# Seven block products in place of eight for the GRU gates of a 64-graph kernel, with block sums on GpSimd and tiles updated in place

## Chip, cores and metric

The kernel runs on one core of one Trainium2 chip. The metric is the device time of one execution in microseconds (us). All runs told of here were in the fast state. A profile of one execution gives the engines' instructions; its "span" is a little shorter than the device time. "Clock" is the share of TensorE's full clock that was granted, and "half clock" is a share of 0.5.

## What is computed

There are 64 graphs of 256 nodes with 256 features, all in fp32. Cut to what matters:

```python
x_conv = relu(bn(conv17(relu(bn(conv1(x))))) + x)           # along the nodes
A = exp(-dist(x @ w_se.T)) * adj
x_nmp = A @ relu(x @ w_msg.T + b_msg)
gi = concat([x_conv, x_nmp]) @ w_ih.T + b_ih                # 512 -> 768
gh = x @ w_hh.T + b_hh                                      # 256 -> 768
r, z = sigmoid(gi_r + gh_r), sigmoid(gi_z + gh_z)
n = tanh(gi_n + r * gh_n)
x1 = layernorm(x + (1 - z) * n + z * x)
h = layernorm(x1, gamma, beta)
out = layernorm(2 * x1 + relu((adj @ h) @ W_rel + b_rel + h @ W_root))
```

## The kernel before

It works in eight rounds of eight graphs. While a round's graphs go through gates, update and aggregation, the convolution of the next round (Winograd-like: many elementwise steps on VectorE, then products on TensorE) is cut into pieces and put between them by `pump()`. The order is made by hand: it is the order in which the program gives each engine, and SyncE, which issues the loads, its instructions.

```python
def load_x(k):                      # on SyncE, like the convolution's weights w
    XG[k] = work.tile([P, C, D], F32, tag="x", name="x")                  # 2 buffers
    nc.sync.dma_start(out=XG[k], in_=x[k].rearrange("(c p) d -> p c d", p=P))

def gates_rz(k, n):                 # n: half of the nodes
    q, ins = inputs(k, n)
    prz = bank("ps_rz")             # one PSUM bank, 512 columns
    for c in range(C):
        nc.tensor.matmul(prz, XT[k][:, c, q], whh[:, c, 0:2 * D], start=(c == 0), stop=False)
    for i, t in enumerate(ins):     # 2 of the convolution, 2 of the messages
        nc.tensor.matmul(prz, t, wih[:, i, 0:2 * D], start=False, stop=(i == 3))
    nc.vector.tensor_add(rz[:, n, :], prz, brzn[:, :2 * D])
    nc.scalar.activation(rz[:, n, :], rz[:, n, :], AF.Tanh, scale=0.5)
# gates_n(k, n): the same with 256 columns for each of gi_n and gh_n ...

def update(k):
    ...
    w = work.tile([P, C, D], F32, tag="w", name="w", bufs=1)
    nc.vector.tensor_sub(w, XG[k], nn)          # the last reader of XG[k]
    ...
    X1[k] = work.tile([P, C, D], F32, tag="x1", name="x1", bufs=2)

# the loop over a round's graphs
    load(k + 3)
    load_x(k + 1)                               # ahead of this graph's convolution weights
    gates_rz(k, 0); pump(); gates_n(k, 0); step(y_left); pump()
    transposes_h(k - 1); pump()                 # its first matmuls mark the stretches below
    gates_rz(k, 1); pump(); passing(k + 1); pump(); factors(k + 2)
    gates_n(k, 1); pump(); project(k - 1)
    ...                                         # update(k), distances, messages, mask
    agg = aggregate(k - 1)                      # y = max(y, 0) + X1[k - 1], late in graph k
```

Of the kernel before, what the change touches and what calls it, by code (L numbers as in the profile page):

```python
# [12 lines left out]
F32 = mybir.dt.float32  # L13
# [16 lines left out]
BG = 8  # L30
NB = B // BG
PI = math.pi

# [41 lines left out]
def gnn_two_layers(  # L75
# [22 lines left out]
    def bank(name):  # L98
        return psum.tile([P, 512], F32, tag="ps", name=name)

    def stt(o, in0, s, in1, op0=ALU.mult, op1=ALU.add):
        nc.vector.scalar_tensor_tensor(o, in0, s, in1, op0=op0, op1=op1)  # L102
# [24 lines left out]
    tb_dram = nc.inline_tensor(np.ascontiguousarray(tb), name="tap_matrix")  # L127
    tap_sb = const.tile([TAPS * OB, NM * OB], F32)
    nc.scalar.dma_start(out=tap_sb, in_=tb_dram.ap())
    mhalf = const.tile([P, 8], F32)  # L130
# [36 lines left out]

    def filters(pool):
        W2[0] = pool.tile([P, C, NM, D], F32, name="w2all")
        pieces, groups = [], []  # L170
# [251 lines left out]
    def conv(b):  # L422
# [97 lines left out]

        xcs = [work.tile([P, C, 4, N], F32, tag="xc", name="xc", bufs=3) for _ in range(2)]

        def channels(q):
            for o in range(C):
                ps = bank("ps_xc")
                for j in range(4):
                    nc.tensor.transpose(ps[:, j * P:(j + 1) * P], X[:, V + 4 * q + j, o * P:(o + 1) * P], ident)  # L527
                pv = ps.rearrange("p (j g t) -> p j g t", j=4, g=BG)
                for h in range(2):
                    nc.scalar.activation(  # L530
                        xcs[h][:, o].rearrange("p g (t j) -> p j g t", j=M)[:, 4 * q:4 * q + 4],
                        pv[:, :, 4 * h:4 * h + 4, :], AF.Relu)
                yield 1.0
# [13 lines left out]
        for g in range(BG):  # L547
            XC[b * BG + g] = (xcs[g // 4], g % 4)


    XG, ADJ, XT, NMP, AT, MSG, X1, H, ST, RZ, OUTS = ({} for _ in range(11))

    def load(k):

        if k >= B:
            return
        XT[k] = work.tile([P, C, N], F32, tag="xT", name="xT", bufs=4)
        nc.sync.dma_start(out=XT[k], in_=xt_dram[k // 2][:, :, (k % 2) * N:(k % 2 + 1) * N])
        ADJ[k] = work.tile([P, C, N], F32, tag="adj", name="adj", bufs=5)
        nc.sync.dma_start(out=ADJ[k], in_=adjT[k].rearrange("(c p) n -> p c n", p=P))  # L560

    def load_x(k):
        if k < B:
            XG[k] = work.tile([P, C, D], F32, tag="x", name="x")
            nc.sync.dma_start(out=XG[k], in_=x[k].rearrange("(c p) d -> p c d", p=P))

    def messages(k):
        MSG[k] = work.tile([P, C, D], F32, tag="msg", name="msg", bufs=3)
        st = work.tile([P, C, 4], F32, tag="st", name="st", bufs=3)
# [37 lines left out]
    def mask(k):  # L607
        nc.vector.tensor_mul(AT[k], AT[k], ADJ[k])
# [9 lines left out]

    def inputs(k, n):
        xc, g = XC[k]  # L620
        q = slice(n * P, (n + 1) * P)
        return q, (xc[:, 0, g, q], xc[:, 1, g, q], NMP[k][:, 0, q], NMP[k][:, 1, q])

    def gates_rz(k, n):
        if n == 0:
            RZ[k] = (work.tile([P, C, 2 * D], F32, tag="rz", name="rz", bufs=1),
                     work.tile([P, C, 2 * D], F32, tag="gn", name="gn", bufs=1))
        q, ins = inputs(k, n)
        prz = bank("ps_rz")
        for c in range(C):  # L630
            nc.tensor.matmul(prz, XT[k][:, c, q], whh[:, c, 0:2 * D], start=(c == 0), stop=False)  # L631
        for i, t in enumerate(ins):
            nc.tensor.matmul(prz, t, wih[:, i, 0:2 * D], start=False, stop=(i == 3))  # L633
        rz = RZ[k][0]

        nc.vector.tensor_add(rz[:, n, :], prz, brzn[:, :2 * D])  # L636
        nc.scalar.activation(rz[:, n, :], rz[:, n, :], AF.Tanh, scale=0.5)  # L637

    def gates_n(k, n):
        q, ins = inputs(k, n)  # L640
        pn = bank("ps_n")
        for c in range(C):
            nc.tensor.matmul(pn[:, D:], XT[k][:, c, q], whh[:, c, 2 * D:], start=(c == 0), stop=(c == C - 1))  # L643
        for i, t in enumerate(ins):
            nc.tensor.matmul(pn[:, :D], t, wih[:, i, 2 * D:], start=(i == 0), stop=(i == 3))  # L645
        nc.vector.tensor_add(RZ[k][1][:, n, :], pn, brzn[:, 2 * D:])  # L646

# [5 lines left out]
    def update(k):  # L653

        rz, gn = RZ[k]
        nn = work.tile([P, C, D], F32, tag="nn", name="nn", bufs=1)
        stt(nn, rz[:, :, :D], 1.0, gn[:, :, D:], op0=ALU.add, op1=ALU.mult)
        stt(nn, nn, 0.5, gn[:, :, :D])
        nc.scalar.activation(nn, nn, AF.Tanh)
        yield  # L660

        w = work.tile([P, C, D], F32, tag="w", name="w", bufs=1)
        nc.vector.tensor_sub(w, XG[k], nn)
        stt(w, rz[:, :, D:], 3.0, w, op0=ALU.add, op1=ALU.mult)
        stt(w, nn, 4.0, w)
        mv = work.tile([P, C, 2], F32, tag="mv", name="mv", bufs=4)
        for n in range(C):
            stats(mv, n, w[:, n, :])


        q = work.tile([P, 2, C], F32, tag="q", name="q", bufs=4)
        nc.gpsimd.tensor_scalar(q[:, 0, :], mv[:, :, 1], 4 * EPS, None, ALU.add)  # L672
        nc.gpsimd.tensor_scalar(q[:, 1, :], mv[:, :, 1], 1 + EPS, 4 * EPS * EPS, ALU.mult, ALU.add)
        nc.gpsimd.tensor_tensor(q, q, mhalf[:, :2 * C].rearrange("p (a c) -> p a c", a=2), ALU.pow)
        sh = work.tile([P, C], F32, tag="sh", name="sh", bufs=4)
        nc.gpsimd.tensor_mul(sh, mv[:, :, 0], q[:, 0, :])
        nc.gpsimd.tensor_scalar(sh, sh, -1.0, None, ALU.mult)
        yield
        H[k] = work.tile([P, C, D], F32, tag="h", name="h", bufs=1)
        X1[k] = work.tile([P, C, D], F32, tag="x1", name="x1", bufs=2)  # L680
        for n in range(C):
            nc.vector.tensor_scalar(H[k][:, n, :], w[:, n, :], mv[:, n, 0:1], q[:, 1, n:n + 1],
                                    ALU.subtract, ALU.mult)
        for n in range(C):
            nc.scalar.activation(X1[k][:, n, :], w[:, n, :], AF.Identity, bias=sh[:, n:n + 1], scale=q[:, 0, n:n + 1])
        yield
# [54 lines left out]
    def step(g):  # L741
        if g is not None:
            next(g, None)
# [3 lines left out]
    with tc.tile_pool(name="first", bufs=1) as first_pool:  # L747
# [22 lines left out]

        brzn = const.tile([P, 4 * D], F32)
        nc.sync.dma_start(out=brzn[:, :3 * D], in_=rows[:, R_IH:R_IH + 3 * D].to_broadcast([P, 3 * D]))
        nc.sync.dma_start(out=brzn[:, 3 * D:], in_=rows[:, R_HH + 2 * D:R_HH + 3 * D].to_broadcast([P, D]))
        bhh = first_pool.tile([P, 2 * D], F32, name="bhh")
        nc.sync.dma_start(out=bhh, in_=rows[:, R_HH:R_HH + 2 * D].to_broadcast([P, 2 * D]))
        gb = const.tile([P, 2, C], F32)
        nc.sync.dma_start(out=gb, in_=rows[:, R_GAMMA:R_GAMMA + 2 * D].rearrange("o (v c p) -> p (o v) c", p=P, c=C))
        whh = weight(whhT, D, 3 * D, "whh", nc.sync)

# [10 lines left out]
        for _ in fl:  # L790
            pass
        nc.vector.tensor_add(brzn[:, :2 * D], brzn[:, :2 * D], bhh)
        nc.gpsimd.tensor_scalar(wrr, wrr, 0.5, None, ALU.mult)
# [4 lines left out]
    work = ctx.enter_context(tc.tile_pool(name="work", bufs=2))  # L798
    wih = weight(wihT, 2 * D, 3 * D, "wih", nc.sync, work)
    for k in range(3):  # L800
        load(k)
    load_x(0)
    early = [lambda: messages(0), lambda: messages(1), lambda: factors(0), lambda: distances(0), lambda: mask(0),
             lambda: factors(1), lambda: distances(1), lambda: mask(1), lambda: passing(0), lambda: messages(2)]
    mark = total
# [5 lines left out]
    for f in early:  # L811
        f()

    POINTS = 10
    y_left = None
    for b in range(NB):
# [12 lines left out]
        for k in range(b * BG, (b + 1) * BG):  # L829
            load(k + 3)  # L830
            load_x(k + 1)
            up = update(k)
            agg = None
            gates_rz(k, 0)
            pump()
            gates_n(k, 0)
            step(y_left)
# [3 lines left out]
            pump()  # L841
            gates_rz(k, 1)
            pump()
            if k + 1 < B:
                passing(k + 1)
            pump()
            if k + 2 < B:
                factors(k + 2)
            gates_n(k, 1)
            pump()  # L850
# [20 lines left out]
        for _ in coming:  # L871
            pass
    step(y_left)
    transposes_h(B - 1)
# [47 lines left out]
```

## Time and profile before

| kernel before | |
|---|---|
| median of 3 runs | 2330.31 us (2328.41 to 2331.38) |
| span, mean granted clock | 2326.0 us, 0.988 |
| busy TensorE, VectorE | 2245.9 us, 1685.6 us |
| half clock between the first transposes of h and the last graph | none |

The busy line, the slices, the chain that ended last and the table by stretches stand in the prediction below. A stretch runs from one graph's transposes of h to the next graph's; there are eight in a round, six in which VectorE is busy for 78 to 96% of the time and two in which it is not.

### The profile page before, as it was taken

How to read it: one execution, taken by the hardware profiler on the slowest of the kernel's cores; microseconds unless marked ns; L12 is line 12 of the kernel's file. 1: busy time of each engine (PE TensorE's matmuls, PEld its weight loads, DVE VectorE, ACT ScalarE, POOL GpSimd, SP SyncE). 2: the span in 40 equal slices, each digit the busy share in tenths (PEclk: the TensorE clock that was granted, in tenths of full speed). 3: DMA queues.
4: the chain of work that ended last, by engine and by line, in shares of the span. 5: the costliest groups of instructions: out<-in, count | busy, mean ns of one | idle time of the engine just before them, and what ended most of it. 6: DMA issues, size and time to landing. Idle time of an engine off the chain costs nothing.

```text
span 2326.0 us, 24209 instructions
## 1 busy us (share of the span) xinstructions
PE 2245.9 (97%) x8262; PEld 1474.6 (63%) x8262; DVE 1685.6 (72%) x3212; ACT 768.0 (33%) x1577; POOL 467.2 (20%) x922
## 2 busy tenths in 40 slices
PE   7779999999999999999999999999999999999996
PEld 4565666656666676666766566666666666666663
DVE  3893988659794788839886597956889298874443
ACT  4514322442224322342224432243223532243332
POOL 1000311212122212202212221222222122121211
PEclk9989999999999999999999999999999999999998
DMA  6543252223322144221522233231432214321100
GB/s 176 164 151 113 74 162 73 84 83 127 118 82 100 50 136 131 75 97 48 170 86 73 100 130 124 73 106 53 136 123 81 100 37 158 107 76 36 46 23 14
DMA packets 211088, 226.66 MB, mean 97 GB/s; under 512 B 22047, under 2 KB 201750, under 8 KB 210966
## 3 DMA queue, kind: packets, MB, share of 16 engines
q1 hardware_dynamic: 188408, 191.14, 25.6%
q10 hardware_dynamic: 22558, 33.99, 4.1%
q8 instruction: 66, 1.08, 0.2%
q14 instruction: 56, 0.46, 0.1%
HBM read 179.22 MB, written 45.88 MB: 97 GB/s over the span
## 4 chain that ended last, share of the span: by engine, by line
PE 80%; DVE 13%; DMA 3%; issue 2%; POOL 1%; ACT 1%; ACTq 0%; SPq 0%; POOLq 0%; DVEq 0%
PE ps_rz L633 17%; PE ps_k L382 11%; PE ps_n L645 9%; PE ps_rz L631 8%; PE ps_out L708 8%; PE ps_c L453 5%; PE ps_nmp L615 5%; PE ps_n L643 4%; DVE XF L102 4%; PE ps_out L720 4%; PE ps_msg L573 4%; PE ps_dist L603 2%; DVE w L102 1%; DVE bst L650 1%; PE ps_xc L527 1%
## 5 line engine op out<-in xcount | busy, mean ns | idle before, releaser
L102 DVE SCALAR_TENSOR_TENSOR XF<-XF 128x512 f32<-128x512 f32 (+2 forms) x800 | 506.8, 664 | 7.0
L672 POOL TENSOR_SCALAR q<-mv 128x2 f32<-128x2 f32 x64 | 32.1, 501 | 1476.0 <-DVE mv L651 1476.0
L382 PE MATMUL ps_k<-w,XF 128*128 128x256 f32 x1316 | 296.8, 382 | 4.3 <-ACT AT L605 1.4
L382 PEld LDWEIGHTS ps_k<-w,XF 128*128 128x128 f32 x1316 | 246.7, 190 | 49.2 <-issue 6.4
L646 DVE TENSOR_TENSOR gn<-ps_n,brzn 128x512 f32<-128x512 f32 x128 | 88.1, 688 | 247.5 <-PE ps_n L645 247.5
L637 ACT ACTIVATE rz<-rz 128x512 f32<-128x512 f32 x128 | 80.6, 630 | 512.8 <-DVE rz L636 512.8
L631 PE MATMUL ps_rz<-whh,xT 128*128 128x512 f32 x512 | 240.7, 592 | 0.0
L633 PE MATMUL ps_rz<-wih,xc 128*128 128x512 f32 x512 | 240.7, 592 | 0.0
L633 PE MATMUL ps_rz<-wih,nmp 128*128 128x512 f32 x512 | 240.6, 592 | 0.0
L708 PE MATMUL ps_out<-wrr,hT 128*128 128x512 f32 x512 | 232.9, 598 | 5.5 <-ACT hT L697 5.5
L636 DVE TENSOR_TENSOR rz<-ps_rz,brzn 128x512 f32<-128x512 f32 x128 | 87.6, 684 | 195.9 <-PE ps_rz L633 195.9
L633 PEld LDWEIGHTS ps_rz<-wih,xc 128*128 128x128 f32 x512 | 97.1, 190 | 122.7 <-issue 121.5
L633 PEld LDWEIGHTS ps_rz<-wih,nmp 128*128 128x128 f32 x512 | 97.3, 190 | 122.4 <-issue 122.4
L708 PEld LDWEIGHTS ps_out<-wrr,hT 128*128 128x128 f32 x512 | 98.1, 192 | 105.2 <-issue 93.0
L573 PE MATMUL ps_msg<-wms,xT 128*128 128x260 f32 x512 | 135.7, 405 | 19.0 <-DVE XF L398 11.0
L577 ACT ACTIVATE msg<-msg 128x512 f32<-128x512 f32 x64 | 40.3, 629 | 343.3 <-DVE msg L576 343.3
L631 PEld LDWEIGHTS ps_rz<-whh,xT 128*128 128x128 f32 x512 | 92.2, 190 | 64.5 <-issue 61.2
L643 PE MATMUL ps_n<-whh,xT 128*128 128x256 f32 x512 | 131.6, 379 | 0.0
L645 PE MATMUL ps_n<-wih,xc 128*128 128x256 f32 x512 | 131.4, 379 | 0.0
L645 PE MATMUL ps_n<-wih,nmp 128*128 128x256 f32 x512 | 131.4, 379 | 0.0
L573 PEld LDWEIGHTS ps_msg<-wms,xT 128*128 128x128 f32 x512 | 95.0, 195 | 53.1 <-issue 23.9
L709 ACT COPY hr<-ps_out 128x256 f32<-128x256 f32 x128 | 47.7, 373 | 242.3 <-PE ps_out L708 242.3
(104 smaller groups left out, 3629.0 us busy)
## 6 DMA issues: line engine op xcount, KB each, us to landing
w<-w2m SPq DMA_DIRECT2D x105, 768.0 KB, 5.9
xn<-in_x_dram SPq DMA_DIRECT2D x32, 512.0 KB, 4.6
xt<-xTc ACTq DMA_DIRECT2D x32, 512.0 KB, 3.3
xT<-xt SPq DMA_DIRECT2D x64, 256.0 KB, 3.0
adj<-in_adjT_dram SPq DMA_DIRECT2D x64, 256.0 KB, 2.8
x<-in_x_dram SPq DMA_DIRECT2D x64, 256.0 KB, 3.0
xb<-in_x_dram SPq DMA_DIRECT2D x32, 512.0 KB, 4.3
out_dram<-y ACTq DMA_DIRECT2D x64, 256.0 KB, 2.2
```

The costliest lines, as they stand in the source:

```text
L102: nc.vector.scalar_tensor_tensor(o, in0, s, in1, op0=op0, op1=op1)
L382: nc.tensor.matmul(ps, X[:, slot, c * P:(c + 1) * P], w(m, c), start=(c == 0), stop=(c == C - 1))
L453: nc.tensor.matmul(ps, w1[:, c, o * P:(o + 1) * P], xTc[:, c, :], start=(c == 0), stop=(c == C - 1))
L573: nc.tensor.matmul(ps[:, :D + 4], XT[k][:, c, m * P:(m + 1) * P], wms[:, c, :], start=(c == 0), stop=(c == C - 1))
L615: nc.tensor.matmul(ps[:, d * N:(d + 1) * N], MSG[k][:, m, d * P:(d + 1) * P], AT[k][:, m, :], start=(m == 0), stop=(m == C - 1))
L631: nc.tensor.matmul(prz, XT[k][:, c, q], whh[:, c, 0:2 * D], start=(c == 0), stop=False)
L633: nc.tensor.matmul(prz, t, wih[:, i, 0:2 * D], start=False, stop=(i == 3))
L643: nc.tensor.matmul(pn[:, D:], XT[k][:, c, q], whh[:, c, 2 * D:], start=(c == 0), stop=(c == C - 1))
L645: nc.tensor.matmul(pn[:, :D], t, wih[:, i, 2 * D:], start=(i == 0), stop=(i == 3))
L646: nc.vector.tensor_add(RZ[k][1][:, n, :], pn, brzn[:, 2 * D:])
L708: nc.tensor.matmul(ps, hT[:, c, n * P:(n + 1) * P], wrr[:, c, :], start=(c == 0), stop=(c == C - 1))
L720: nc.tensor.matmul(po, ADJ[k][:, m, n * P:(n + 1) * P], hr[:, m, :], start=False, stop=(m == C - 1), skip_group_check=True)
```

## The change

The intent is to save TensorE time. The gates are a product of a 256-row left side and a 256-row weight, seen as 2 x 2 blocks of 128; a Strassen-type form needs seven block products in place of eight. It needs sums of left blocks (put on GpSimd), differences of weight blocks (once, at the start) and sums of products (VectorE, out of PSUM, where the kernel's banks for TensorE's products lie). To make room, the GRU update works in place, and the convolution's result goes to a ring of 10 graphs. Core of the diff, with cuts:

```diff
 def load_x(k):
-    XG[k] = work.tile([P, C, D], F32, tag="x", name="x")
+    XG[k] = work.tile([P, C, D], F32, tag="x", name="x", bufs=3)
+def blocks(src, s1, s2, s3, s4):
+    a11, a12, a21, a22 = (src[:, c, n * P:(n + 1) * P] for n in range(C) for c in range(C))
+    nc.gpsimd.tensor_add(s1, a21, a22)
+    nc.gpsimd.tensor_sub(s2, s1, a11)
+    nc.gpsimd.tensor_sub(s3, a11, a21)
+    nc.gpsimd.tensor_sub(s4, a12, s2)
+    return a11, a12, s4, a22, s1, s2, s3
+def block_product(k, i, ps, start):        # nmp and xc 384 columns each, x 256
+    for j, (name, w) in enumerate((("nmp", wg[:, i, 1, :]), ("x", wx[:, i, :]), ("xc", wg[:, i, 0, :]))):
+        nc.tensor.matmul(ps[:, :w.shape[-1]], LEFT[k, name][i], w, start=start and j == 0, ...)
+def gates(k):
+    a = bank("ps_a"); block_product(k, 0, a, True)
+    nc.vector.tensor_add(g00, a[:, :HG], bg[:, 1, :])
+    d = bank("ps_d"); block_product(k, 1, d, True)
+    nc.vector.tensor_add(g00, g00, d[:, :HG])
+    yield
+    b_ = bank("ps_b"); block_product(k, 4, b_, True)
+    nc.scalar.copy(g11, b_[:, :HG])
+    c_ = bank("ps_c"); block_product(k, 6, c_, True)
+    nc.vector.tensor_add(g11, g11, c_[:, :HG])
+    yield
+    block_product(k, 5, a, False)              # the fifth, onto bank a: needs the first add to be done
+    nc.vector.tensor_add(<g01 and g10>, <a twice>, bg)
+    ...                                        # products 2 onto b_, 3 onto c_
 def update(k):
-    w = work.tile([P, C, D], F32, tag="w", name="w", bufs=1)
-    nc.vector.tensor_sub(w, XG[k], nn)
+    w = XG[k]
+    nc.vector.tensor_sub(w, w, nn)
     ...
-    X1[k] = work.tile([P, C, D], F32, tag="x1", name="x1", bufs=2)
+    X1[k] = w
...
+    for i, j, l in ((6, 2, 4), (4, 4, 0), (5, 2, 4), (3, 1, 5)):      # at the start
+        for w in (wg, wx):
+            nc.gpsimd.tensor_sub(w[:, i], w[:, j], w[:, l])
```

## The prediction

> **What bounds the kernel now.** I read the page's busy table first, then the slices, then the chain that ended last, and then asked for what no average tells: the busy time of each engine in stretches of one round.
>
> ```profile
> PE 2245.9 (97%) x8262; PEld 1474.6 (63%) x8262; DVE 1685.6 (72%) x3212; ACT 768.0 (33%) x1577; POOL 467.2 (20%) x922
> ...
> PE   7779999999999999999999999999999999999996
> ...
> DVE  3893988659794788839886597956889298874443
> ...
> PE 80%; DVE 13%; DMA 3%; issue 2%; POOL 1%; ACT 1%; ACTq 0%; SPq 0%; POOLq 0%; DVEq 0%
> ```
>
> TensorE is busy 97% of the span, 80% of the final chain is its own work, and the only slices below 9 are the first three (filters, first convolution) and the last. So a microsecond of TensorE work removed from the steady part is worth a microsecond, as long as nothing else takes over. VectorE at 72% looks like room. But its digits swing between 4 and 9, so I cut one round of eight graphs at its eight transposes of h (at 509.92, 535.95 and so on) and asked for the stretches. Columns: us of the stretch; busy us of TensorE, its weight loads, VectorE, ScalarE, GpSimd; clock; DMA.
>
> ```profile
> 509.92:535.95 26.03, 26.03 (x91) 16.26 (x90) 24.87 (x43) 8.38 (x17) 8.31 (x16) 1.00 0.12 41
> 535.95:572.60 36.65, 36.64 (x140) 25.25 (x139) 35.00 (x61) 10.69 (x21) 11.90 (x19) 1.00 0.46 147
> 572.60:616.58 43.98, 42.34 (x163) 29.69 (x162) 37.81 (x82) 9.71 (x20) 7.37 (x14) 1.00 0.42 134
> 616.58:658.42 41.84, 40.98 (x160) 29.10 (x158) 33.69 (x72) 9.71 (x20) 8.03 (x14) 1.00 0.31 104
> 658.42:684.45 26.03, 26.03 (x91) 16.26 (x90) 23.35 (x51) 7.18 (x16) 4.81 (x10) 1.00 0.24 79
> 684.45:713.11 28.66, 28.66 (x115) 18.79 (x114) 25.14 (x47) 12.51 (x27) 9.32 (x18) 1.00 0.21 74
> 713.11:740.89 27.78, 27.78 (x108) 17.96 (x107) 11.86 (x28) 12.81 (x28) 5.62 (x16) 1.00 0.23 76
> 740.89:783.63 42.74, 42.66 (x149) 24.93 (x147) 16.73 (x23) 19.15 (x38) 4.52 (x8) 1.00 0.29 99
> ```
>
> The reader should see two kinds of stretch. In the last two TensorE is full and VectorE is at 43% and 39%. In the first six VectorE is busy 179.9 of 203.2 us, in the first two 96%. Seven of the eight rounds look like this; the last one has no next convolution, VectorE at 46% and 26.03 us per graph.
>
> [...] The trace has two MATMULs per fp32 product and these starts:
>
> ```profile
> 919.12 1.88 PE L631 MATMUL ps_rz<-whh,xT 128*128 128x512 f32 x4
> 920.84 1.88 PE L633 MATMUL ps_rz<-wih,xc 128*128 128x512 f32 x4
> 922.55 1.88 PE L633 MATMUL ps_rz<-wih,nmp 128*128 128x512 f32 x4
> 924.27 1.03 PE L643 MATMUL ps_n<-whh,xT 128*128 128x256 f32 x4
> 925.13 1.03 PE L645 MATMUL ps_n<-wih,xc 128*128 128x256 f32 x4
> ```
>
> Start to start this is 1.716 us per four, 0.429 us each at 512 columns, and 0.2165 us each at 256: linear[...]. [...]
>
> ```profile
> 705.74 1.22 DVE L538 TENSOR_TENSOR XF<-XF,xb 128x1024 f32<-128x1024 f32 x1
> ...
> 705.96 1.05 POOL L582 TENSOR_TENSOR ns<-sq 128x2 f32<-128x2 f32 x1
> ```
>
> A two-element GpSimd sum, 0.19 us when free, took 1.05 us and ended 0.05 us after VectorE's two-input add ended at 706.96. [...]
>
> **Part 1, TensorE.** Before, one graph's gates are 24 instructions of 512 columns and 24 of 256: 24 x 0.429 + 24 x 0.2165 = 15.5 us. After, each of seven products has four of 384 (interpolated 0.323) and two of 256: 1.725 us, times 7 = 12.08; the part of h in the n gate stays, 8 x 0.2165 = 1.73. Sum 13.81. Saved: **1.69 us per graph, 108 us for 64**, all of it on the engine that sets the end. If nothing else moved: 2222 us.
>
> **Part 2, VectorE.** Removed: four evictions of 512 columns (0.686 us each, 2.74) and the two products for h (0.37 each busy, 0.73), which go to ScalarE. Added: the blocks must be summed out of PSUM: five evictions or adds of 384 columns from PSUM and one in SBUF (0.55, between 0.416 at 256 and 0.686 at 512, so 3.3), one of 768 (0.96) and one of 512 (0.69): 4.95. Net **+1.47 us per graph**, 94 us over the run.
>
> **Part 3, GpSimd.** Twelve two-input sums of 128 columns per graph. [...] I take **1.5 us**.
>
> **Part 4, ScalarE.** A copy of 384 columns and two normalisations more, about +1.7 us on a 33% engine: hidden, except that h now goes GpSimd, then ScalarE: about 1 us later.
>
> **Part 5, start.** The new weights need four differences of 768 and four of 256 columns on GpSimd, queued ahead of the first graph's small sums (which ran at 164.6 us) on which its distances, mask and messages hang. [...] **about +12 us**, nothing hidden, since TensorE is idle there. The ring of convolution results and the in-place tiles only free memory.
>
> **Sum.** Crowded six stretches: TensorE 203.2 - 6 x 1.69 = 193.1. VectorE 179.9 + 6 x (1.47 + 1.5) = 197.7, already over TensorE, so these end at about 198 to 200, a gain of 3 to 5 in place of 10. The two light ones gain 3.4. Per round 6.5, seven rounds 45; the last round's eight graphs the full 13.5; the start -12. Gain 46: **2284, say 2285 us**.
>
> **Rivals.** (a) TensorE stays the bound and VectorE's lag is absorbed in the light stretches: 108 less 12 less some waits, 2240 to 2255. For: GpSimd never visibly delayed VectorE before. Against: the new accumulation reuses bank a, so the fifth product waits for VectorE's first eviction some 6 us earlier in TensorE's order, while at the crowded graphs VectorE begins that eviction (of rz) already 6 us after its matmul. TensorE can no longer run far ahead. (b) VectorE becomes the bound[...]: the crowded stretches get longer than before and only light graphs gain, 2310 to 2330. (c) GpSimd's queue delays its own normalisation sums, and h comes late to its transposes, which have only 2 to 4 us to spare at some graphs: same size as (b).
>
> **Range and chances.** Between (a) and (b): 2245 to 2325. A gain of 2% is 2283.7, in the middle of it; the change clearly removes work from the bound, so slower by 2% is remote. Faster 0.47, same 0.49, slower 0.04.
>
> **What would show it.** Gate matmuls at 0.323 us start to start and TensorE busy down by 100 us or so; VectorE busy up by 94 us or more, its two-input instructions longer than 0.69 us at 512 columns where block sums run (this decides between a and b); TensorE waits "from VectorE" or "from GpSimd" in the first stretches of a round, none in the light ones; the first gate matmul at about 200 us, where it was at 188. I am wrong if VectorE's durations do not change and TensorE has no new waits (then 2245), or if block sums take a microsecond each and starve the gates (then above 2325).

The 1.5 us per graph for VectorE held by GpSimd's sums, some 10 of the 12 us of the start, and the size of rival (b) were estimates, and the sum keeps them: it set VectorE at 197.7 us in the six crowded stretches and came to a gain of 46 us, 2285 us. What the trace before does show is a sum on GpSimd that took 0.19 us at 185.19 and 1.05 us at 705.96, beside VectorE's add; that add took 1.22 us, and the mean of such steps of 1024 columns is 1.215, so VectorE was not seen to be held there. ScalarE's 1.7 us can be worked out from the same trace: two normalisations of 0.59 us each, and a copy of 384 columns put at 0.5 from the 0.37 us at 256.

## More of the kernel before

One more view matters later, SyncE's waits before it can issue a transfer (line of the transfer, what it waited for, us in total, times, longest). Before:

```profile
SPq L377 <- DMA w<-w2m: 62.3, 14, 5.0
SPq L565 <- DVE w L663: 59.5, 3, 25.6
```

Line 565 is the load of x. It waited three times in the whole run. Line 377 is the load of the convolution's weights w, which stands behind it in the queue.

## The result

| | before | changed |
|---|---|---|
| median | 2330.85 us (4 runs) | 2413.70 us (4 runs, 2406.36 to 2427.85) |
| span, clock | 2326.0 us, 0.988 | 2404.5 us, 0.965 |
| TensorE busy, idle | 2245.9, 80.1 us | 2190.2, 214.3 us |
| half clock in the steady part | 0 | 81.9 us in 19 stretches |

The ratio is 1.0365 (95% interval 1.0316 to 1.0413): slower, outside the predicted range. A ratio here and below is the mean time of one kernel's fast runs over that of the other's of the same rounds, so not quite the ratio of the quoted medians. The changed kernel is correct.

The page of the changed kernel, busy times, slices and the chain:

```profile
PE 2190.2 (91%) x8390; PEld 1524.7 (63%) x8390; DVE 1831.0 (76%) x3340; ACT 853.2 (35%) x1745; POOL 864.6 (36%) x1698
...
PE   7868899998999989999999998999999999999997
...
PE 44%; DVE 42%; DMA 5%; issue 5%; POOL 2%; ACT 2%; SPq 0%; DVEq 0%; ACTq 0%; POOLq 0%
```

TensorE has 8s in the middle of the row where it had none, and its share of the chain has fallen from 80% to 44%, while VectorE's rose from 13% to 42%. The second round by stretches, cut at the same transposes (us of the stretch; busy us of TensorE, weight loads, VectorE, ScalarE, GpSimd; clock; DMA):

```profile
535.90:566.30 30.40, 27.83 (x93) 18.39 (x93) 27.85 (x46) 11.12 (x23) 17.23 (x29) 0.89 0.11 35
566.30:611.20 44.90, 37.95 (x142) 27.55 (x141) 39.28 (x69) 11.77 (x25) 17.39 (x30) 0.92 0.40 127
611.20:654.80 43.60, 40.80 (x166) 29.99 (x165) 37.73 (x78) 11.14 (x23) 13.06 (x26) 1.00 0.41 134
654.80:697.40 42.60, 39.46 (x161) 29.36 (x160) 37.07 (x73) 11.14 (x23) 14.26 (x26) 1.00 0.34 107
697.40:721.70 24.30, 24.30 (x93) 16.64 (x92) 23.64 (x47) 9.16 (x20) 11.39 (x22) 1.00 0.08 23
721.70:753.80 32.10, 29.06 (x118) 20.57 (x117) 28.55 (x51) 13.85 (x31) 16.54 (x30) 0.95 0.32 107
753.80:781.50 27.70, 26.34 (x111) 18.25 (x109) 13.28 (x29) 13.73 (x30) 10.28 (x28) 1.00 0.24 77
781.50:822.90 41.40, 41.18 (x151) 25.01 (x148) 18.86 (x26) 18.98 (x39) 8.97 (x20) 1.00 0.29 96
```

The fifth stretch (24.30 us, 26.03 before) shows the intended gain. The first, second and sixth lost 4, 8 and 3 us, and there VectorE is not at its limit either: in the second, TensorE is idle for 7 of 44.9 us while VectorE is idle for 5.6. The clock is under 1.00 in three stretches; before it was 1.00 everywhere. TensorE's waits, of the whole run:

```profile
PE ps_k L384 <- DMA w<-w2m: 54.5, 19, 5.4
PE ps_a L653 <- DVE g L664: 41.2, 20, 2.4
PE ps_sT L601 <- POOL st L593: 22.0, 1, 22.0
```

The second and third were in the prediction (bank a, and the start). The first was not. Its largest case stands in the second stretch. SyncE's issues there, then TensorE, then VectorE's step that ended just before, then the stretches of 4 us around it, where the clock is the third column from the right:

```profile
585.78 0.37 SPq L569 DMA_DIRECT2D adj<-in_adjT_dram  x1
591.36 0.37 SPq L574 DMA_DIRECT2D x<-in_x_dram  x1
591.77 1.77 SPq L379 DMA_DIRECT2D w<-w2m  x3
```

```profile
590.75 0.81 PE L653 MATMUL ps_c<-wg,nmp 128*128 128x384 f32 x2
591.39 0.59 PE L653 MATMUL ps_c<-wx,xsum 128*128 128x256 f32 x2
591.83 0.81 PE L653 MATMUL ps_c<-wg,xc 128*128 128x384 f32 x2
598.04 5.46 PE L384 MATMUL ps_k<-w,XF 128*128 128x256 f32 x12 [5.41 <-DMA w<-w2m]
```

```profile
590.60 0.69 DVE L104 SCALAR_TENSOR_TENSOR y<-y,x 128x512 f32<-128x512 f32 x1
```

```profile
590.00:594.00 4.00, 2.63 (x10) 1.41 (x8) 3.69 (x10) 2.44 (x5) 3.14 (x11) 1.00 0.35 87
594.00:598.00 4.00, 0.00 (x0) 0.00 (x0) 3.96 (x3) 1.09 (x2) 2.38 (x1) 0.82 1.00 336
598.00:602.00 4.00, 3.96 (x9) 3.20 (x10) 3.71 (x4) 0.00 (x0) 0.00 (x0) 0.50 0.86 288
602.00:606.00 4.00, 4.00 (x17) 3.40 (x16) 0.00 (x0) 0.58 (x1) 0.00 (x0) 0.82 0.29 59
```

Read them together. SyncE issued `adj` at 585.78 and then nothing until 591.36, when it issued `x`, 0.07 us after VectorE's step `y<-y,x` had ended (590.60 + 0.69). That step is the last reader of an in-place x tile, which now serves as x, as w and as x1 until late in the next graph. The three weight transfers stand behind `x` and went out at 591.77; TensorE was out of work at 592.6 and stood for 5.41 us. In the clock column (1.00, 0.82, 0.50, 0.82) the clock is then at half for 6.8 us, from 596.6 on. The first group also shows the gate products at the predicted rate: 0.64 us for two instructions of 384 columns, 0.44 for two of 256.

In the view of SyncE's waits, the load of x is now held 61 times:

```profile
SPq L574 <- DVE y L104: 272.6, 61, 23.1
```

That is a theory of the loss from one place: in-place x, an early place in the queue, weights behind it. The rivals were those of the prediction (VectorE as the bound, slowed by GpSimd's sums, and bank a). The experiments tell them apart.

### The profile page after: what moved, and what is told of

It is laid out like the page before. It is cut to its first block, busy times and chain, and to the rows that moved or that the text cites. A ratio compares the mean times of both kernels' runs of the same rounds, so it can differ in the third digit from the quotient of the medians.

```text
span 2404.5 us, 25743 instructions
## 1 busy us (share of the span) xinstructions
PE 2190.2 (91%) x8390; PEld 1524.7 (63%) x8390; DVE 1831.0 (76%) x3340; ACT 853.2 (35%) x1745; POOL 864.6 (36%) x1698
## 4 chain that ended last, share of the span: by engine, by line
PE 44%; DVE 42%; DMA 5%; issue 5%; POOL 2%; ACT 2%; SPq 0%; DVEq 0%; ACTq 0%; POOLq 0%
DVE XF L104 14%; PE ps_k L384 10%; PE ps_c L653 5%; PE ps_b L653 5%; PE ps_a L653 4%; PE ps_c L455 4%; PE ps_n L696 3%; PE ps_nmp L624 3%; DVE x L104 3%; DVE bst L703 3%; PE ps_out L760 3%; DMA w<-w2m 2%; DVE XF L465 2%; DVE XF L361 2%; DVE XF L303 1%
## 5 line engine op out<-in xcount | busy, mean ns | idle before, releaser
L384 PE MATMUL ps_k<-w,XF 128*128 128x256 f32 x1316 | 315.5, 399 | 60.2 <-DMA w<-w2m 54.5
L361 DVE TENSOR_TENSOR XF<-XF 128x512 f32<-128x512 f32 (+3 forms) x128 | 127.0, 1014 | 1.8
L677 DVE TENSOR_TENSOR g<-ps_a,bg 128x768 f32<-128x768 f32 x64 | 61.0, 953 | 86.5 <-PE ps_a L653 86.5
L455 PE MATMUL ps_c<-xTc,w 128*128 128x512 f32 x256 | 118.4, 605 | 8.8 <-ACT xTc L447 8.8
L624 PE MATMUL ps_nmp<-AT,msg 128*128 128x256 f32 x512 | 122.8, 383 | 0.0
L772 PE MATMUL ps_out<-hr,adj 128*128 128x256 f32 x512 | 122.3, 381 | 0.1
L696 PE MATMUL ps_n<-wn,xT 128*128 128x256 f32 x512 | 121.1, 379 | 0.0
L749 ACT ACTIVATE hT<-ps_hT,gb 128x256 f32<-128x256 f32 x128 | 65.0, 558 | 152.6 <-PE ps_hT L747 139.3
L624 PEld LDWEIGHTS ps_nmp<-AT,msg 128*128 128x128 f32 x512 | 98.3, 192 | 27.8 <-issue 1.0
L653 PE MATMUL ps_b<-wg,xcsum 128*128 128x384 f32 x256 | 104.6, 491 | 9.5 <-POOL xcsum L634 9.5
L788 ACT ACTIVATE y<-y,sh,q 128x256 f32<-128x256 f32 x128 | 69.9, 593 | 109.0 <-POOL sh L785 109.0
```

What stands on the lines that cost most here:

```text
L361: (nc.vector.tensor_add if add else nc.vector.tensor_sub)(sl(o, n), sl(a, n), sl(b, n))
L384: nc.tensor.matmul(ps, X[:, slot, c * P:(c + 1) * P], w(m, c), start=(c == 0), stop=(c == C - 1))
L455: nc.tensor.matmul(ps, w1[:, c, o * P:(o + 1) * P], xTc[:, c, :], start=(c == 0), stop=(c == C - 1))
L624: nc.tensor.matmul(ps[:, d * N:(d + 1) * N], MSG[k][:, m, d * P:(d + 1) * P], AT[k][:, m, :], start=(m == 0), stop=(m == C - 1))
L653: nc.tensor.matmul(ps[:, :w.shape[-1]], LEFT[k, name][i], w, start=start and j == 0, stop=j == 2, skip_group_check=not start)
L696: nc.tensor.matmul(ps[:, n * D:(n + 1) * D], XT[k][:, c, n * P:(n + 1) * P], wn[:, c, :], start=(c == 0), stop=(c == C - 1))
```

## The experiments

"Start" is the time of the first transposes of h (236.6 us before, 254.4 changed). All runs were timed beside the kernel before (2330 to 2332 us). The edits are to the changed kernel if nothing else is said.

### The queue: e1_x_late, b1_in_place, b2_in_place_x_late

e1 moves one line of the changed kernel; b1 puts into the kernel before only the in-place tile; b2 is b1 with the load moved too.

```diff
 # e1: in the loop over graphs
     load_adj(k + 2)
-    load_x(k + 1)
...
     passing(k + 1)
     pump()
+    load_x(k + 1)
     step(ga)
```

```diff
 # b1: kernel before, in update() and load_x(); b2 moves load_x(k + 1) behind factors(k + 2)
-XG[k] = work.tile([P, C, D], F32, tag="x", name="x")
+XG[k] = work.tile([P, C, D], F32, tag="x", name="x", bufs=3)
-w = work.tile([P, C, D], F32, tag="w", name="w", bufs=1)
-nc.vector.tensor_sub(w, XG[k], nn)
+w = XG[k]
+nc.vector.tensor_sub(w, w, nn)
-X1[k] = work.tile([P, C, D], F32, tag="x1", name="x1", bufs=2)
+X1[k] = w
```

> Only change to the changed kernel: the load of the next graph's x is issued in the middle of a graph instead of at its start, so that it no longer stands in the transfer queue ahead of the convolution's weights while its buffer is still in use. Theory Q (queue): the 54.5 us in which TensorE waited for w, and part of the lowered clock behind those gaps, go away by themselves: 2340 to 2360 us, TensorE's wait for w under 10 us. Theory V (VectorE, held up by GpSimd's sums, is the bound there and the wait for w only hides it): the waits reappear as waits for VectorE and the time stays at 2395 or more.

> The kernel BEFORE with one part of the change alone: the update and x1 are written over the x tile (3 buffers), as in the changed kernel; gates, sums and h stay as before. Theory Q1 (the in-place x tile alone blocks the transfer queue): TensorE waits 20 us or more for w, where it waited 0.9, and the time rises to 2350 to 2385. Theory Q2 (the blocked queue hurts only together with VectorE's extra work): wait for w under 10 us and 2325 to 2342.

> The kernel before with the in-place x tile (2412 alone) and x loaded in the middle of a graph. Theory Q1 says that the in-place tile costs nothing but the blocked queue: wait for w back to under 5 us, no lowered clock after the start, 2322 to 2342. If in-place updates cost something else as well (instructions waiting for each other on one tile), 2355 or more.

| run | median us | ratio to before | half clock, steady |
|---|---|---|---|
| e1_x_late | 2343.28 | 1.0047 (1.0019 to 1.0075) | 58.0 us |
| b1_in_place | 2411.80 | 1.0347 (1.0330 to 1.0364) | 37.5 us |
| b2_in_place_x_late | 2324.46 | 0.9971 (0.9953 to 0.9988) | 3.4 us |

All three are correct. The waits of b1, first TensorE's, then SyncE's:

```profile
PE ps_k L382 <- DMA w<-w2m: 55.0, 21, 5.1
```

```profile
SPq L565 <- DVE y L102: 369.9, 61, 25.6
```

b1 has none of the seven products and none of GpSimd's sums, and it alone loses 81 us, with the same wait for w (55.0 us, 21 times; 54.5 and 19 in the changed kernel). It came at 2412 us, where 2350 to 2385 was expected. Moving the one line takes all of it back, and 6 us more than that. In the changed kernel the same move gives 70 us, and TensorE's wait for w falls from 54.5 to 2.1 us. So the loss is not the products': a tile that lives longer is enough, with the weights behind its load in SyncE's queue (`x` at 591.36 above, `w` at 591.77). The length of the queue's wait alone says little: in b2 the load of x is still held for 270.9 us in 41 cases (59.5 in 3 before), and in e1 for 207.4 us in 41, and the weights for TensorE are no longer behind it when it matters.

### GpSimd's block sums: e3_no_sums, e7_no_sums_x_late

Their outputs are wrong, which doesn't matter for the times. After graph 0 the left sides are taken from the blocks and from graph 0's old sums, so that GpSimd does no sums and all other work stays. e7 has x later as well.

```diff
 def sums(k, name):
+    if k > 0:
+        src = {"x": XT, "nmp": NMP, "xc": XC}[name][k]
+        ...                                     # a11, a12, a21, a22 of src
+        LEFT[k, name] = (a11, a12, old[2], a22, old[4], old[5], ...)
+        return
```

> WRONG RESULT ON PURPOSE: from the second graph on the block sums are not formed, the products take the first graph's sums; everything else is as in the changed kernel. It measures what the twelve sums per graph cost. Theory V: VectorE's 128x512 two-input steps fall back from 762 to 686 ns, VectorE's busy time falls by 40 us or more and the time by 50 us or more (under 2365). Theory Q: the sums cost little, the waits for w stay above 40 us, and the time falls by less than 30 us (above 2385).

> WRONG RESULT ON PURPOSE: x loaded later, and no block sums after the first graph. With the queue out of the way it tells what the sums on GpSimd cost. If they hold VectorE up by 0.8 us per graph and that is on the path: 2285 to 2305, and the wait for bank a falls below 25 us. If the rest is VectorE's own added instructions: 2325 or more.

e3: 2368.74 us, ratio 1.0156 (1.0139 to 1.0174); e7: 2304.64 us, ratio 0.9889 (0.9872 to 0.9905). So the sums cost 45 us with the queue as it was and 39 us with it put right. e3 fell between its two theories (under 2365 or over 2385; TensorE's wait for w went to 36.9 us, where 40 or more was expected of theory Q). e7 came inside its range, but its wait for bank a stayed at 40.1 us, where under 25 was expected. VectorE's busy time fell by 50 to 56 us in both. Its 512-column convolution steps, in the groups by form, of before, of e1 (with sums) and of e7 (without):

```profile
L102 DVE SCALAR_TENSOR_TENSOR XF<-XF 128x512 f32<-128x512 f32 x448 | 294.6, 686 | 5.0
```

```profile
L104 DVE SCALAR_TENSOR_TENSOR XF<-XF 128x512 f32<-128x512 f32 x448 | 326.9, 754 | 5.0
```

```profile
L104 DVE SCALAR_TENSOR_TENSOR XF<-XF 128x512 f32<-128x512 f32 x448 | 302.9, 701 | 5.0
```

The mean of one step is 686 ns before, 754 with the sums and 701 without them. So VectorE's steps take longer while GpSimd does the sums (the hold): 50 to 56 us over 64 graphs is 0.8 to 0.9 us per graph, where the prediction took 1.5. The sums themselves, in the changed kernel:

```profile
L634 POOL TENSOR_TENSOR xsum<-xT 128x128 f32<-128x128 f32 x64 | 46.2, 722 | 501.1 <-PE ps_b L653 501.1
L635 POOL TENSOR_TENSOR nmpsum<-nmpsum,nmp 128x128 f32<-128x128 f32 x64 | 30.4, 476 | 5.0
```

The shortest kind takes 476 ns on average, the others up to 722 ns for the same 128 columns; why is not shown.

### The start: e2_start, e8_diff_dve

e2 puts GpSimd's weight differences behind the first small sums, with the old queue; e8 does them on VectorE in their old place, with x later.

```diff
 # e2                                           # e8
-for i, j, l in (...): nc.gpsimd.tensor_sub     -nc.gpsimd.tensor_sub(w[:, i], w[:, j], w[:, l])
+early = [messages(0), messages(1),             +nc.vector.tensor_sub(w[:, i], w[:, j], w[:, l])
+         differences, factors(0), ...]
```

> Only change to the changed kernel: the eight differences of gate weights on GpSimd come after the small sums of the first two graphs instead of before them. If those differences are what delays the first gates, the 22 us wait of TensorE for st goes to a few us and the time falls by 12 to 18 us (2396 to 2402). If the 13 weight transfers are the cause, less than 5 us.

> The changed kernel with x loaded later (2343) and the eight weight differences on VectorE in place of GpSimd. [...]GpSimd's 13.5 us of differences held up VectorE's steps one by one; on VectorE they should take about 5.5 us: time down by 6 to 10 us (2333 to 2338), first gates earlier by as much. If the start is bound by the weight transfers, no change (2340 or more).

e2: 2409.57 us, ratio 1.0336 (1.0318 to 1.0354), 4 us under the changed kernel, where 12 to 18 was expected, and not clear of noise (the runs of both kernels overlap). The wait for the small sums fell from 22.0 to 6.4 us, but TensorE then waited 13.7 us for a convolution step that VectorE was late with. VectorE, then GpSimd (cut), then the busy times of 13 us:

```profile
169.52 14.24 DVE L104 SCALAR_TENSOR_TENSOR XF<-XF 128x512 f32<-128x512 f32 x10
```

```profile
174.29 2.25 POOL L873 TENSOR_TENSOR wg<-wg 128x768 f32<-128x768 f32 x1
176.50 1.17 POOL L873 TENSOR_TENSOR wx<-wx 128x256 f32<-128x256 f32 x1
```

```profile
171.00:184.00 13.00, 3.36 (x8) 1.29 (x7) 12.93 (x9) 2.36 (x6) 13.00 (x8) 0.50 0.00 1
```

Ten steps that take 0.686 us each in the kernel before took 14.24 us, 7.4 more, beside eight GpSimd subtractions that follow each other without a gap (13.7 us in all, from 170.86 on; so the delay was about half of their time, as far as the profile's rough spans on GpSimd tell). On VectorE the eight take 5.5 us in e8 (four of 955 ns, four of 419), on GpSimd 13.5 in the changed kernel. e8: 2338.29 us, ratio 1.0027 (1.0009 to 1.0045), start 246.6; e1's was 250.5. So 4 to 5 us seem to come back when the differences leave GpSimd, but this is not clear of noise: the two intervals overlap, and one profiled start differs from another by as much with the same instructions (h3 249.8 us, h4 245.7, below).

### Bank a and the places of the work: e4_three_fixes, e5_p5_later, e6_spread

With the queue put right, e1's largest wait is for bank a: 49.4 us in 20 cases, all in the first, second and sixth stretch of a round. Three tries to take it away:

```diff
 # e4 (x later, e2's start, and:)          # e5 (x later, and in gates():)          # e6 (x later, and:)
     transposes_h(k - 1); pump()            +block_product(k, 2, b_, False)          -PE_WEIGHT = 0.3
+    gates_n(k)                              block_product(k, 5, a, False)           +PE_WEIGHT = 0.1
     step(ga)  # fifth product              ...                                      # in channels()
...                                         -block_product(k, 2, b_, False)          -yield 1.0
-    gates_n(k)                                                                      +yield 0.3
```

> The changed kernel with three edits: x loaded later, weight differences after the first small sums, and the n gate's product moved ahead of the fifth block product, so that TensorE has 1.7 us more before it needs bank a back from VectorE. Theory Q: 2414 less about 65 (w), 15 (start) and 10 to 20 (bank a): 2310 to 2330, level with the kernel before or just under it. Theory V: above 2370.

> The changed kernel with x loaded later (2343), and the product that goes on in bank b put before the one that goes on in bank a, so that TensorE asks for bank a 1.7 us later. If bank a is a cause of its own: its 49 us of waits fall by 20 or more and the time to 2310 to 2325. If VectorE is the bound in the crowded stretches, the wait moves to another instruction and the time stays within 2335 to 2350.

> The changed kernel with x loaded later, and the convolution's TensorE-only steps weighted less in the pacing (0.1 and 0.3 in place of 0.3 and 1.0), so that its VectorE steps spread over more of the eight graphs of a round. If VectorE is the bound only because its work is crowded into six of eight graphs: 2285 to 2320, bank-a waits and lowered clock both at half or less. If it makes no odds where the steps lie: 2335 to 2350.

e4: 2342.26 us, ratio 1.0045 (1.0028 to 1.0062); e5: 2348.27, 1.0077 (1.0060 to 1.0093); e6, which spreads the convolution's work differently over the round: 2368.88, 1.0163 (1.0147 to 1.0178). None beats e1 by more than 1 us. e4 missed its 2310 to 2330; e5 stayed where VectorE as the bound would have it (2335 to 2350); e6 lies above both of its ranges, and why was not followed up. The wait for bank a did shrink in e4; its two largest waits:

```profile
PE ps_dist L612 <- ACT lr L604: 45.3, 26, 3.0
PE ps_a L653 <- DVE g L664: 17.2, 16, 1.9
```

49.4 us became 17.2, and another wait grew from 7.5 us (e1) to 45.3. The time did not follow the wait, so bank a alone was not the cause. That VectorE is, which is busy for 88 to 98% of these three stretches (lines of e8 below), is argued here; the hybrid tests it.

### Seven products only where VectorE has room: h1, h2, h3, h4

The hybrid keeps one weight block more from h3 on (the tiles AT and y have one buffer to make room for it) and makes the gates of a graph in either form; eight products go each to a bank of their own, with no sums and no return to a bank. It has e8's queue, and the differences on VectorE, from h3 on behind the first small sums.

```diff
+def seven(k):
+    return k >= B - BG or k % BG in (0, 3, 4, 5, 7)    # h2, h3; h1: (0, 7); h4: 2 as well
 def sums(k, name):
+    if not seven(k):
+        return
+def gates_eight(k):
+    for n in range(C):
+        for h in range(2):
+            ps = bank("ps_e")
+            block(k, n, h, ps)                         # two block products, summed in PSUM
+            nc.vector.tensor_add(g[:, n, h, :], ps[:, :HG], bg[:, 1 - h, :])
+            if h == 1:
+                nc.scalar.activation(<row n of g>, AF.Tanh, scale=0.5)
+            yield
```

> As e8, but graphs 1 to 6 of each of the first seven rounds, where VectorE is crowded, take eight block products (each in its own bank, no block sums, no return to a bank) and only graphs 0 and 7 and the last round take seven. If the crowding is what eats the gain: 22 graphs keep 1.69 us each (37), less about 5 at the start: 2290 to 2305, few waits and little lowered clock. If seven products don't pay at all: 2325 or more.

> As h1, with seven products in graphs 0, 3, 4, 5 and 7 of a round, eight in 1, 2 and 6, the three places where the changed kernel with x loaded later was slower than before. If those three are the only places where VectorE binds: 43 graphs keep 1.69 us (73), less 5 to 15: 2265 to 2285. If the waits only move on: 2300 or more.

> The changed kernel with x loaded later, the weight differences on VectorE, and B12 kept as an eighth weight block, so that both forms are right: seven products in graphs 0, 3, 4, 5 and 7 of each of the first seven rounds and in the whole last round, eight products (no block sums, no return to a bank) in the others. It is the same choice as h2, with right weights. Theory (seven products pay where VectorE has room, and cost where it is full): correct, 2275 to 2292 us, about 1.8% under before. Rival (the choice gained only because h2 read a wrong weight block, or the eighth block's room costs time): over 2300.

> As h3, with graph 2 of the first seven rounds on seven products too. If graph 2 has VectorE time to spare: 7 x 1.7 = 12 us less than h3 at most, 1 to 5 likely. If VectorE binds there, the extra sums cost more than the matmuls save: equal to h3 or some us slower.

| run | seven products in graphs | median us | ratio to before |
|---|---|---|---|
| h1 (wrong result) | 0, 7, and the last round | 2321.33 | 0.9960 (0.9945 to 0.9974) |
| h2 (wrong result) | 0, 3, 4, 5, 7, and the last round | 2288.52 | 0.9820 (0.9803 to 0.9836) |
| h3 | as h2 | 2285.73 | 0.9803 (0.9790 to 0.9816) |
| h4 | as h3, and 2 | 2295.77 | 0.9843 (0.9830 to 0.9857) |

h1 and h2 gave wrong results by a mistake: the block they used for eight products had been overwritten by a difference. The same instructions run, and h3, with the right block kept, has about the same time.

h1 missed its 2290 to 2305: the two light stretches gained little (the seventh 27.71 us, where eight products take 27.80; the eighth 42.03 where they take 42.63), though VectorE has room there. The step from h1 to h2 is made by graphs 3, 4 and 5, where VectorE is busy for 80 to 90% before and each graph gains its whole 1.7 us. h2 is 3.5 us over its range, h3 within it. One graph more on seven products (h4) costs 10 us: the second stretch goes from 36.47 to 37.55 us in the mean of the seven rounds, 7.6 us in all, and the wait for bank a is back with 13.2 us in 7 cases.

### Eight products in the same kernel: h0_eight_all, h0b_tanh_later

What are the products worth when all the rest of the change is there? h0 is the hybrid with eight products everywhere.

```diff
 # h0                          # h0b, besides: the first tanh one block later
 def seven(k):                 -if h == 1:
+    return False              -    nc.scalar.activation(<row n of g>, AF.Tanh, scale=0.5)
                               +if n == 1:
                               +    nc.scalar.activation(<row h of g>, AF.Tanh, scale=0.5)
```

> As h3, with eight products in every graph: what the seven products are worth when all else is the same. Against it stand e8 (seven everywhere, 2338 us) and h3 (seven where VectorE has room). Theory: 2322 to 2332, so that seven everywhere lose some 6 to 16 us of their own and seven in five of eight graphs gain 35 to 50. Rival (the loss left in e8 is the in-place tiles', the ring's or the later load's, not the products'): h0 near or over 2338.

> The kernel with eight products in every graph (2360 us) lost 22 to 25 us to one place of my own making: in six rounds ScalarE did a tanh and the last normalisation just when the next convolution's transposed x was to be copied, TensorE stood 2.0 us and its clock was halved for 3.4 us after. Here the first tanh comes one block later. Theory (that wait is an accident of the order, and eight products with all the rest of the change equal stand at about before plus the longer start): 2335 to 2342, the stretch after every eighth transpose of h back from 46.5 to about 42.8 us; then seven products everywhere (2338) gain nothing over eight. Rival (the wait was not the cause): 2355 to 2362.

h0 took 2360.44 us, ratio 1.0122 (1.0108 to 1.0136), on the side of its rival (near or over 2338), not of its theory (2322 to 2332). But its stretches differ from the kernel before by more than 0.5 us in the last one only, 46.3 in place of 42.7 us. TensorE there, and the clock after (0.91, 0.66):

```profile
760.69 3.23 PE L455 MATMUL ps_c<-xTc,w 128*128 128x512 f32 x4 [2.02 <-ACT xTc L447]
```

```profile
758.00:762.00 4.00, 1.98 (x9) 1.00 (x7) 0.00 (x0) 3.13 (x6) 0.00 (x0) 0.91 0.51 178
762.00:766.00 4.00, 4.00 (x8) 1.67 (x7) 0.00 (x0) 1.59 (x4) 0.00 (x0) 0.66 0.38 150
```

ScalarE had a tanh and a normalisation to do just when the next convolution's x was to be copied. TensorE waited for 2.02 us and then ran at half clock for 3.4. h0b moves that tanh: 2340.09 us, ratio 1.0036 (1.0023 to 1.0048), the last stretch 42.63 us. So h0's extra 20 us were an accident of my order, and the confounded run is replaced by h0b.

### The start once more: h5_start

h5 is h3 with graph 0 of the run on eight products, and the differences at the end of the start.

```diff
-    return k >= B - BG or k % BG in (0, 3, 4, 5, 7)
+    return k >= B - BG or k > 0 and k % BG in (0, 3, 4, 5, 7)
-early = [messages(0), messages(1), differences, factors(0), ...]
+early = [messages(0), messages(1), factors(0), ...]
 ...
 sums(0, "xc")
+differences()
```

> The kernel with seven products where VectorE has room (2286 us), graph 0 of the run on eight products too, so that the weight differences can stand behind the filters on VectorE and hold nothing at the start. Theory (the differences' 6 us and the wait of 10 us for the convolution result are what makes its start 13 us longer than before's): first transposes of h at about 240 instead of 249.8 us, time 2274 to 2280. Rival (the start is longer because of the 13 small weight transfers or the later x): no change, 2284 to 2289.

It is correct: **2279.33 us, ratio 0.9774 (0.9760 to 0.9787)**, faster than both kernels. Start 243.0 us (h3: 249.8). The first, second and sixth stretch of its second round, then those of e8 (seven everywhere):

```profile
512.12:538.61 26.49, 26.33 (x99) 17.87 (x99) 25.61 (x45) 10.68 (x22) 8.43 (x18) 1.00 0.14 41
538.61:575.08 36.47, 36.47 (x147) 26.82 (x146) 34.30 (x56) 11.30 (x23) 14.10 (x30) 1.00 0.47 148
...
681.08:710.28 29.20, 29.00 (x123) 20.25 (x121) 27.08 (x49) 12.46 (x28) 18.25 (x31) 1.00 0.33 100
```

```profile
520.02:548.86 28.84, 26.27 (x94) 17.55 (x94) 28.19 (x46) 11.07 (x24) 17.79 (x29) 0.94 0.12 37
548.86:586.43 37.57, 35.22 (x142) 25.71 (x141) 36.54 (x62) 11.71 (x25) 17.39 (x30) 1.00 0.47 155
...
693.79:727.54 33.75, 30.29 (x116) 20.82 (x117) 29.59 (x54) 14.98 (x33) 17.72 (x34) 0.90 0.27 86
```

In h5 TensorE is full in these stretches and the clock is 1.00, though it has more products to do (147 matmul records against 142 in the second). In e8 VectorE has 2 to 3 us more to do in each, TensorE is idle for 2.4 to 3.5 us, and the clock drops in two of the three.

Two summaries, the mean length of each stretch over five rounds, and what the runs make of the 83 us:

| kernel | start | 1 | 2 | 3 | 4 | 5 | 6 | 7 | 8 | round | last-round graph |
|---|---|---|---|---|---|---|---|---|---|---|---|
| before | 236.6 | 26.03 | 36.46 | 43.42 | 42.18 | 26.03 | 28.66 | 27.78 | 42.73 | 273.3 | 26.03 |
| changed | 254.4 | 28.72 | 43.56 | 44.32 | 42.53 | 24.33 | 31.61 | 27.71 | 41.78 | 284.6 | 24.33 |
| e8, seven everywhere | 246.6 | 28.96 | 36.90 | 41.48 | 40.21 | 25.40 | 33.05 | 27.70 | 41.41 | 275.1 | 24.33 |
| h0b, eight everywhere | 246.8 | 26.49 | 36.76 | 43.11 | 41.93 | 26.05 | 28.68 | 27.80 | 42.63 | 273.4 | 26.05 |
| h5, seven in five of eight | 243.0 | 26.49 | 36.44 | 41.46 | 40.21 | 24.33 | 29.19 | 27.77 | 41.59 | 267.5 | 24.33 |

| step | us | from |
|---|---|---|
| changed kernel to e1: x later in the queue | -70 | 2413.7 to 2343.3 |
| e1 to e8: differences off GpSimd (not clear of noise) | -5 | 2343.3 to 2338.3 |
| e8 to h0b: eight in place of seven everywhere (not clear of noise) | +2 | 2338.3 to 2340.1 |
| h0b to before: longer start | -8 | 2340.1 to 2332.2; start 246.8 to 236.6 |

The steps make 81 us, as the kernel before took 2332.2 us in the last of these runs. With the queue put right, seven products in every graph are worth about nothing over eight (2 us): in seven rounds they lose 1.7 us each (275.1 to 273.4), and in the last they gain 8 x 1.72.

## Why the prediction was wrong, and where it was right

- **What failed first is the sentence "The ring of convolution results and the in-place tiles only free memory."** The in-place x tile alone costs 81 us (b1), and the place of its load is worth 70 us in the changed kernel (e1). Nothing in the sum stood for it. It is not all of the miss, since e1 at 2343 us is still outside the range. In the trace of the changed kernel the load that waits for its buffer holds what stands behind it on SyncE: nothing from 585.78 on, then `x` at 591.36 and `w` at 591.77. It could have been asked beforehand: who reads the new tile last, and what stands behind its load?
- **TensorE's saving was right.** Gate instructions take 0.32 and 0.22 us, and a graph with no other limit goes from 26.03 to 24.33 us, 1.70 against 1.69 predicted. Busy TensorE fell by 55.7 us only, not 108, as 81.9 us went by at half clock: at most half of that, 41 us, is work that took twice as long (two gate instructions of 384 columns, start to start: 1.28 us at half clock, from 541.66 on, and 0.64 at full clock, from 590.75 on). Of the other 11 us some is the start's, which had 63.9 us at half clock where it had 37.5 before; the rest is open.
- **"TensorE idle" was counted as idle time only.** Neither the sum nor a rival of the prediction allowed for a lower clock. In the changed kernel's steady part 14 stretches at half clock were 3.4 us long and 5 were 6.8 us. All 7 gaps of TensorE of more than 3 us (4.06 to 5.40) had one that began between 2.0 us before and 1.1 us after the end of the gap, and so had 7 of 28 gaps of 1.8 to 3 us (those 7 were of 2.11 to 2.42 us, the half clock from 0.8 us before to 1.4 us after their end); in h0 about 3.4 us at half clock came with a gap of 2.02 us. The other 5 stretches began 1.7 to 2.4 us after a gap of 1.1 us, the largest in the 8 us before. So in these runs the length of a gap alone does not tell whether half clock follows. No such stretch was counted in the steady part of h3, h5 and h0b (in h5's second round the clock is 1.00 in all eight stretches). The clock's share was not isolated by a run: it always came with the gaps.
- **VectorE's extra was there, but smaller than said.** +145 us busy (1831.0 against 1685.6), where 64 x (1.47 + 1.5) = 190 was predicted; the sums' hold was 0.8 to 0.9 us per graph, not 1.5. With the queue put right, VectorE's busy time in the six crowded stretches is 194.4 us in e8, under the predicted 197.7.
- **"So these end at about 198 to 200" failed all the same.** The six crowded stretches of e8 take 206.0 us. The step took one sum over six stretches, and so assumed that VectorE could be packed to 99%; it is busy for 94%. That is 7 us per round, 49 in all. The prediction's own figures, taken stretch by stretch, would have told half of it: the larger of VectorE + 2.97 and TensorE - 1.69 is 27.8, 38.0, 42.3, 40.2, 26.3 and 28.1 us, together 202.7, with VectorE over TensorE in the first, second, fifth and sixth. For the rest there are TensorE's waits for bank a (48.7 us in 20 cases) and 54.7 us at half clock in e8's steady part, at most 27 us of delay; how they divide it is not shown. Without the sums (e7) the six take 202.6 us, so the hold is not all of it either. The two light ones gave 1.4 us per round in place of 3.4: in the seventh, TensorE waits 1.4 us for GpSimd's sums of the convolution (h5: 9.5 us in 7 cases).
- **The start** was 17.8 us longer (12 predicted); e8 shows 10 without the differences on GpSimd, h5 6.4 with them moved out. A start can scatter by 4 us (h3 249.8, h4 245.7).
- **Rivals.** Rival (b), VectorE as the bound and only light graphs gain, 2310 to 2330, is nearest to what remains once the queue is put right: e1 and e8 are at 2343 and 2338, a little above. Rival (a) fell. Rival (c), late h, hardly showed: TensorE waited for h 11.5 us in 8 cases in the changed kernel and 6.8 us in 2 before, about 5 us of each at the end of the run. The wait for bank a that the prediction named was there in the 20 cases of the three fullest stretches, but e4 and e5 suggest that it is a place where the lag shows, not its cause.

Open: how much of the time lost per gap is the clock's, and whether another order in the first, second and sixth stretch could make seven products pay there too.

## What to carry to other kernels

An in-place update lengthens a buffer's life: look for the load that refills it, and for what stands behind that load in its queue; with the wrong place, saving the room of two tiles cost 81 us here. Before trading work from the bounding engine to another, cut the trace into stretches, compare the two engines in each, and make the trade only where the other engine has room (needed, but not enough: in the two light stretches the gain was small all the same). Seven products everywhere gained 2 us, seven in five of eight graphs gained 61 us (h5 against h0b, some of it from the start). A wait that moves when you take it away, while the time stays, was not the cause by itself; look at the engine behind it.
